# First attention: dense q and k projections, spread over the partitions through DRAM

## The chip, the cores and the metric

The kernel runs on one core of one Trainium2 chip. Its time is the device time of one execution in microseconds (us). Three runs of the kernel before took 4,061.84, 4,043.44 and 4,053.35 us; the median is 4,053.35. The profile shows one further execution, taken by the hardware profiler.

The engines are TensorE (PE, with its weight loads as PEld), VectorE (DVE), ScalarE (ACT), GpSimd (POOL) and SyncE (SP, whose queue issues the DMAs here).

## The reference

The network takes `x` of 2 batch rows, 1,024 tokens and 128 features, and runs eight sublayers over it, each on a layer norm of `x` and each added to `x`: a windowed attention (`attn_a`), a mixture of experts, a causal attention, the experts again, an attention with positions, a six-layer local-attention network, another attention, and the six-layer network again. The change is in the first sublayer, which is, cut to what matters:

```python
W, H = 64, 16; dh = D // H                       # D = 128, so dh = 8
q = x @ Wq.T + bq;  k = x @ Wk.T + bk;  v = x @ Wv.T + bv
kp = pad(k, W rows in front);  vp = pad(v, W rows in front)
idx = arange(C)[:, None] * W + arange(2 * W)[None, :]
scores = einsum('bcqhd,bckhd->bchqk', q by windows, kp[:, idx]) / sqrt(dh)
scores = where(idx >= W, scores, -1e9)
out = einsum('bchqk,bckhd->bcqhd', softmax(scores), vp[:, idx])
return out @ Wo.T + bo
```

Each window of 64 tokens looks at itself and the window before it, with 16 heads of 8 features. All arithmetic is in 32-bit floats.

## The kernel before

`x` is held transposed, features on the 128 partitions, as four blocks of 512 tokens (`self.xt`, two blocks for each batch row). Three early stages use the same small constants, loaded by `load_early` (L108): `self.w["a0"]` holds all weights of the first attention side by side.

`attn_a0` (L207) has two parts. The first part goes over the four blocks (L233 and L234). For each block:

- `norm` (L147) makes the layer norm. It transposes the block to token rows on PE (L158), takes means and variances on DVE (L162, L163), a root on ACT (L172) and a reciprocal on DVE (L173), scales four pieces on DVE (L181), transposes back on PE (L190) and copies the result to `xn` on ACT (L193).
- q and k are made for four groups `g` of four heads each (L236 to L246). A product gives one group: 128 output rows, of which head `j` of the group takes rows 32j to 32j + 7. The other 24 rows of each 32 are zero, since the weights were laid out so on the host (`spread`, L1780, in `_layout`). q leaves PSUM by way of ACT (L239), k by way of DVE (L244), into tiles `qT` and `kT`, indexed partition, group, token. So a block takes eight products, four for q and four for k.
- v is made with tokens on the partitions, in eight products of 128x128 (L250), and leaves by way of DVE (L254).

The PSUM tiles of the products (`pq`, `pk`, `pv`) share four buffers with the scores that follow. The order of the instructions in this part is the planner's own: it follows the program and takes an instruction ahead when its inputs are ready. On PE the order of a block is: transposes out of block k, transposes in of block k + 1, the products of q and k, and those of v.

The second part is `Chunks.run` (L834), under an order written out by the loop itself, the same on PE, ACT, DVE and POOL. It handles 16 chunks of 128 tokens, eight for each batch row. A chunk's `scores` (L854, products at L869) read q and k at partitions 32j to 32j + 7 only, one small product for each head and half; `softmax` (L874) subtracts the maxima on DVE and takes the exponential on ACT; `sums` (L886) normalises with POOL; then come transposes, the products with v (`outputs`, L907) and every four chunks the output product (`project`, L922). Chunks 0 to 3 read the first block of the first batch row, chunks 4 to 7 the second (and the last 64 keys of the first), and so on. PE reaches the scores of chunk 0 after the last product of v of the fourth block.

SP's queue is not in the written orders. It issues the loads of `x` (L128) and of the constants (L101) at the start; its next instructions belong to the experts' stage (L1097, L1102).

Of the kernel before, what the change touches and what calls it, by code (L numbers as in the profile page):

```python
# [10 lines left out]
F32 = mybir.dt.float32  # L11
BF16 = mybir.dt.bfloat16
AF = mybir.ActivationFunctionType
ALU = mybir.AluOpType
# [3 lines left out]
P = 128  # L18
B, N, D = 2, 1024, 128
# [6 lines left out]
HEADS, DH, WIN = 16, 8, 64  # L26
# [58 lines left out]
class Net:  # L85
# [118 lines left out]

    def attn_a0(self, key):  # L207
        nc, tc = self.nc, self.tc
        scale = 1.0 / math.sqrt(DH)
        with ExitStack() as ctx:  # L210
            wp = ctx.enter_context(tc.tile_pool(name="a0w", bufs=1))
            sb = ctx.enter_context(tc.tile_pool(name="a0s", bufs=2))
            ps = ctx.enter_context(tc.tile_pool(name="a0ps", bufs=2, space=PSUM))
            wp2 = ctx.enter_context(tc.tile_pool(name="a0av", bufs=1, space=PSUM))
            w, bv, mask = self.w["a0"], self.w["a0_bv"], self.w["a0_mask"]
            wqk = w[:, 0:1024].rearrange("p (s g e) -> p s g e", s=2, g=4)
            wv = w[:, 1024:1152]
            wo = w[:, 1152:1664].rearrange("p (g e) -> p g e", g=4)
            bqk = w[:, 1664:1672].rearrange("p (s g) -> p s g", s=2)
            bo = w[:, 1672:1673]  # L220

            def blk(b, k):
                return slice(WIN + 512 * k, WIN + 512 * (k + 1))

            xn, qT, kT, v = [], [], [], []
            for b in range(B):
                xn.append(wp.tile([P, WIN + N], F32, tag=f"xn{b}", name=f"a0xn{b}"))
                qT.append(wp.tile([P, 4, N], F32, tag=f"q{b}", name=f"a0q{b}"))
                kT.append(wp.tile([P, 4, WIN + N], F32, tag=f"k{b}", name=f"a0k{b}"))
                v.append(wp.tile([P, N // WIN, D], F32, tag=f"v{b}", name=f"a0v{b}"))  # L230
                nc.gpsimd.memset(xn[b][:, 0:WIN], 0.0)
                nc.gpsimd.memset(kT[b][:, :, 0:WIN], 0.0)
            for b in range(B):  # L233
                for k in range(2):  # L234
                    self.norm(self.xt[2 * b + k], xn[b][:, blk(b, k)], ps, f"{key}_{b}_{k}")
                    for g in range(4):  # L236
                        pq = ps.tile([P, 512], F32, tag="sc", name=f"a0pq{b}{k}{g}", bufs=4)
                        nc.tensor.matmul(pq, wqk[:, 0, g, :], xn[b][:, blk(b, k)], start=True, stop=True)
                        nc.scalar.activation(  # L239
                            qT[b][:, g, ts(k, 512)], pq, AF.Identity, bias=bqk[:, 0, g : g + 1]  # L240
                        )
                        pk = ps.tile([P, 512], F32, tag="sc", name=f"a0pk{b}{k}{g}", bufs=4)
                        nc.tensor.matmul(pk, wqk[:, 1, g, :], xn[b][:, blk(b, k)], start=True, stop=True)
                        nc.vector.tensor_scalar(  # L244
                            kT[b][:, g, blk(b, k)], pk, bqk[:, 1, g : g + 1], None, ALU.add
                        )  # L246
                    for c4 in range(2 * k, 2 * k + 2):
                        pv = ps.tile([P, 4, D], F32, tag="sc", name=f"a0pv{b}{c4}", bufs=4)
                        for c in range(4):
                            nc.tensor.matmul(  # L250
                                pv[:, c, :], xn[b][:, ds(WIN * (4 * c4 + c), 2 * WIN)], wv,
                                start=True, stop=True,
                            )
                        nc.vector.tensor_tensor(  # L254
                            v[b][:, ts(c4, 4), :], pv, bv[:, None, :].to_broadcast([P, 4, D]), ALU.add
                        )

            avs = [wp2.tile([P, 4, P], F32, tag=f"av{i}", name=f"a0av{i}") for i in range(2)]
            for av in avs:
                nc.vector.memset(av, 0.0)  # L260
            with tc.manual_schedule(engines=ORDERED):
                Chunks(self, qT, kT, v, wo, bo, avs, mask, scale, sb, ps).run()

# [1501 lines left out]
def _columns(v, width=P):  # L1767

    v = np.asarray(v)
    out = np.zeros((-(-v.size // width) * width,), v.dtype)  # L1770
    out[: v.size] = v
    return out.reshape(-1, width).T


def _layout(a):
    f = np.float32
    t = {"x": a["L0_attn_a_x"].reshape(T, D)}


    def spread(v):  # L1780
        out = np.zeros((4, 4, 32) + v.shape[1:], f)
        out[:, :, :DH] = v.reshape((4, 4, DH) + v.shape[1:])
        return out.reshape((4, P) + v.shape[1:])

    n = "L0_attn_a_"
    wqk = [spread(a[n + w]).transpose(2, 0, 1).reshape(P, 512) for w in ("Wq", "Wk")]
    t["a0"] = np.concatenate(
        wqk + [a[n + "Wv"].T, spread(a[n + "Wo"].T).transpose(1, 0, 2).reshape(P, 512)]
        + [spread(a[n + v]).T for v in ("bq", "bk")] + [_columns(a[n + "bo"])],
        1,  # L1790
    )
    t["a0_bv"] = a[n + "bv"].reshape(1, D)

    n = "L0_ffn_"
    w123 = [a[n + w].transpose(2, 0, 1).reshape(D, E * P) for w in ("w1", "w2", "w3")]
    sw3 = a[n + "sw3"].T.reshape(2, P, D).transpose(1, 0, 2).reshape(P, 2 * D)
    desc = np.tile(np.arange(E, 0, -1, dtype=f), (P, 1))
    t["f0"] = np.concatenate(
        w123 + [a[n + "sw1"].T, a[n + "sw2"].T, sw3, a[n + "gate_w"].T, a[n + "b1"].T, a[n + "b2"].T, desc,
         a[n + "b3"].T],  # L1800
        1,
    )
    t["b0"] = np.concatenate([a["L0_attn_b_wqk"], a["L0_attn_b_wov"]], 1)

    n = "L1_attn_a_"
    heads = np.repeat(np.eye(HEADS, dtype=f), DH, axis=0)
    t["a1"] = np.concatenate(
        [a[n + w] for w in ("Wq", "Wk", "Wv", "Wo")]
        + [_columns(a[n + "bq"]), _columns(a[n + "bo"])]
        + [np.tile(a[n + "pos_emb"][0, :, 0:3], (HEADS, 1)), heads],  # L1810
        1,
    )
    t["a1_rows"] = np.concatenate([a[n + v] for v in ("bq", "bk", "bv")]).reshape(1, 3 * D)

    n = "L1_attn_b_"

    t["b1_a"] = np.stack([np.repeat(a[n + m + "A"].transpose(1, 0, 2), 32, axis=0) for m in "qkvo"], 1)
    t["b1_s"] = np.stack([np.tile(a[n + m + "S"].transpose(1, 0, 2), (4, 1, 1)) for m in "qkvo"], 1)
    t["b1_gains"] = np.concatenate([a[n + "g1"], a[n + "b1"]]).reshape(1, 2 * D)
    t["b1_rows"] = np.concatenate([a[n + v] for v in ("qb", "kb", "vb")]).reshape(1, 3 * D)  # L1820
    t["b1_cols"] = np.concatenate([_columns(a[n + v]) for v in ("g1", "b1", "g2", "b2", "ob")], 1)

    for n in ("Wo", "W1", "W2"):
        t[n] = a[f"L1_ffn_{n}"]

    w = a["L1_ffn_Wqkv"]
    wv = w[:, :, 2 * INNER :].reshape(DEPTH, D, LH // 4, 2, 2 * LD).transpose(0, 1, 3, 2, 4)

    wqk = w[:, :, : 2 * INNER].reshape(DEPTH, D, 2, LH, 2, LD // 2).transpose(0, 1, 2, 4, 3, 5)
    t["Wqkv"] = np.concatenate(  # L1830
        [wqk.reshape(DEPTH, D, 2 * INNER), wv.reshape(DEPTH, D, INNER)], 2
    )
    qs, ks = a["L1_ffn_q_scale"], a["L1_ffn_k_scale"]
    roll = lambda v: np.roll(v, LD // 2, axis=-1)
    t["qk_scale"] = np.concatenate([qs, ks, roll(qs), roll(ks)], -1)
    b1 = a["L1_ffn_b1"]
    t["f1_cols"] = np.stack(
        [
            np.concatenate(
                [  # L1840
                    _columns(b1[i, :DI]), _columns(b1[i, DI:]), _columns(a["L1_ffn_ln_g"][i]),
                    _columns(a["L1_ffn_ln_b"][i]), _columns(a["L1_ffn_b2"][i]),
                ],
                1,
            )
            for i in range(DEPTH)
        ],
        1,
    )
    return t  # L1850
# [18 lines left out]
```

## Time and profile before

| what | value |
|---|---|
| median of three runs | 4,053.35 us (4,043.44 to 4,061.84) |
| the profiled execution's own time | 4,040.27 us |
| its span in the trace | 4,038.5 us |
| mean granted TensorE clock | 0.963 |
| start to the first norm's products (0 to 18.5 us) | PE busy 7.24 us |
| projections of the four blocks (18.5 to 58.9 us) | PE busy 39.25 us of 40.4 |
| chunk loop (58.9 to 232 us) | PE busy 130.74, DVE 136.22 of 173.1 us |
| everything after (232 to 4,038.5 us) | PE busy 3,684.7 us |

Times in the trace are from the span's start. A group or a piece of a timeline gives start, length, engine, line, operation, the tile written and the tiles read, and how many instructions were merged; in square brackets stands how long the engine had been idle and what ended the idle time. A row of windows gives the stretch, its length, the busy time of PE, PEld, DVE, ACT and POOL with the number of instructions, the granted TensorE clock, the busy share of the DMA engines and GB/s. The chain of waits goes back from the last instruction, at each step to what released it. A 32-bit product shows as two PE instructions.

### The profile page before, as it was taken

The page shows a single profiled execution, that of the slowest core. Times are in us where ns is not written, and L with a number is a line of the kernel's source. Part 1 is how long each engine was busy: PE and PEld are TensorE (multiplying, and loading weights), DVE is VectorE, ACT ScalarE, POOL GpSimd, SP SyncE. Part 2 cuts the span into 40 slices and gives each one's busy share as a digit, 9 for nine tenths or more (in the row PEclk, how much of TensorE's full clock was granted, in tenths as well). Part 3 has the DMA queues.
Part 4 walks back from the last instruction along what each step waited for, and adds up shares of the span by engine and source line. Part 5 has one row for each costly group of instructions (what it writes and reads, how often), then busy time and mean ns, then how long its engine had stood idle before and what let it go on. Part 6 is the DMA issues. An engine that isn't in the chain of part 4 may idle for free.

```text
span 4038.5 us, 156175 instructions
## 1 busy us (share of the span) xinstructions
PE 3861.9 (96%) x67340; PEld 2533.3 (63%) x67340; DVE 3140.5 (78%) x6016; ACT 2429.7 (60%) x4600; POOL 2495.8 (62%) x1614
## 2 busy tenths in 40 slices
PE   7889988999999999999999869999999999999998
PEld 4545544666666666666666536666666666666665
DVE  6866677787878787878788677787878787778786
ACT  3444435866666666666666448666666666566665
POOL 1333247776676766766766267766766767667662
PEclk8689888999999999999999879999999999999999
DMA  1011213332232333322222022333322323332222
GB/s 48 2 49 36 56 29 105 73 85 71 74 93 68 77 84 76 82 73 73 70 68 68 21 81 71 75 84 76 85 72 72 91 69 76 82 75 70 65 68 56
DMA packets 215541, 277.31 MB, mean 69 GB/s; under 512 B 52173, under 2 KB 108362, under 8 KB 214730
## 3 DMA queue, kind: packets, MB, share of 16 engines
q1 hardware_dynamic: 214858, 267.32, 25.9%
q8 instruction: 536, 8.78, 1.0%
q14 instruction: 147, 1.20, 0.1%
HBM read 67.76 MB, written 1.18 MB: 17 GB/s over the span
## 4 chain that ended last, share of the span: by engine, by line
PE 88%; DVE 6%; DMA 2%; ACT 1%; issue 1%; POOL 1%; SPq 0%; DVEq 0%; POOLq 0%; ACTq 0%
PE pj_l L1353 17%; PE y_l L1584 9%; PE pv_l L1455 9%; PE tqk_l L201 9%; PE av_l L1552 8%; PE sc_l L1502 7%; PE tpr_l L201 4%; PE to_l L201 4%; PE fg_l L1658 3%; PE fy_l L1694 3%; PE fa_l L1679 3%; PE sc_l L1493 2%; DMA f0share_e<-f0d_e 1%; PE f0F_e L1144 1%; PE f0S_e L1144 1%
## 5 line engine op out<-in xcount | busy, mean ns | idle before, releaser
L1382 DVE TENSOR_TENSOR t_l<-pj_l,rot_l 128x512 f32<-128x512 f32 x1536 | 968.3, 684 | 368.1 <-ACT sq_l L1362 356.5
L1399 POOL TENSOR_TENSOR raw_l<-t_l,t_l 128x1024 f32<-128x1024 f32 x384 | 909.0, 2367 | 532.5 <-DVE on_l L1560 307.1
L1353 PE MATMUL pj_l<-wqkv_l,x_l 128*128 128x512 f32 x1536 | 786.0, 614 | 7.0 <-DVE t_l L1382 4.8
L1414 POOL TENSOR_TENSOR raw_l<-raw_l,rn_l 128x1024 f32<-128x1024 f32 x384 | 723.7, 1903 | 94.7 <-ACT rn_l L1409 87.8
L1362 ACT ACTIVATE sq_l<-pj_l 128x512 f32<-128x512 f32 x768 | 462.4, 604 | 370.2 <-PE pj_l L1353 368.3
L1388 POOL TENSOR_TENSOR sq_l<-sq_l 128x512 f32<-128x512 f32 x384 | 491.5, 1280 | 311.2 <-ACT sq_l L1362 308.2
L201 PE MATMUL tqk_l<-ident_sb,raw_l 128*128 128x128 f32 x3072 | 453.1, 279 | 15.6 <-POOL raw_l L1414 13.6
L1432 ACT COPY qT_l<-tqk_l 128x512 f32<-128x512 f32 x384 | 225.3, 587 | 388.1 <-PE tqk_l L201 388.0
L201 PEld LDWEIGHTS tqk_l<-ident_sb,raw_l 128*128 128x128 f32 x3072 | 356.8, 142 | 160.6 <-issue 122.0
L1455 PE MATMUL pv_l<-wqkv_l,x_l 128*128 128x512 f32 x768 | 415.2, 623 | 5.7 <-DVE ln_xn_fl L1638 5.3
L1584 PE MATMUL y_l<-outT_l,wo_l 128*128 128x128 f32 x3072 | 393.7, 281 | 0.0
L1502 PEld LDWEIGHTS sc_l<-kT_l,qT_l 64*32 64x32 f32 x24576 | 294.7, 105 | 156.4 <-issue 146.0
L1584 PEld LDWEIGHTS y_l<-outT_l,wo_l 128*128 128x128 f32 x3072 | 357.5, 191 | 18.2 <-issue 1.0
L1552 PE MATMUL av_l<-vw_l,pT_l 64*32 64x64 f32 x24576 | 359.9, 224 | 6.0 <-issue 5.8
L1353 PEld LDWEIGHTS pj_l<-wqkv_l,x_l 128*128 128x128 f32 x1536 | 255.8, 192 | 172.6 <-issue 108.9
L1464 ACT COPY v_l<-pv_l 128x512 f32<-128x512 f32 x384 | 225.5, 587 | 222.4 <-PE pv_l L1455 201.7
L1560 DVE TENSOR_TENSOR on_l<-av_l,inv_l 128x512 f32<-128x512 f32 x384 | 247.5, 686 | 124.0 <-PE av_l L1552 123.7
L1552 PEld LDWEIGHTS av_l<-vw_l,pT_l 64*32 64x32 f32 x24576 | 294.0, 105 | 74.0 <-issue 67.6
L1502 PE MATMUL sc_l<-kT_l,qT_l 64*32 64x64 f32 x24576 | 329.1, 223 | 1.4 <-issue 1.4
L201 PEld LDWEIGHTS tpr_l<-ident_sb,pr_l 128*128 128x128 f32 x1536 | 188.9, 141 | 152.4 <-issue 117.5
L1512 DVE TENSOR_TENSOR pr_l<-sc_l,mx_l 128x512 f32<-128x512 f32 x384 | 265.6, 692 | 13.2
L1511 DVE TENSOR_REDUCE mx_l<-sc_l 128x8 f32<-128x512 f32 x384 | 261.6, 681 | 3.4 <-PE sc_l L1502 3.4
(321 smaller groups left out, 6177.7 us busy)
## 6 DMA issues: line engine op xcount, KB each, us to landing
vw_l<-v_l SPq DMA_DIRECT2D x3024, 64.0 KB
wqkv_l<-in_Wqkv SPq DMA_DIRECT2D x36, 512.0 KB
f0share_e<-f0d_e SPq DMA_DIRECT2D x64, 256.0 KB
rot_l<-in_rotary SPq DMA_DIRECT2D x24, 512.0 KB
wo_l<-in_Wo SPq DMA_DIRECT2D x12, 512.0 KB
w_l<-in_W SPq DMA_DIRECT2D x12, 341.0 KB
f_sb<-in_f SPq DMA_DIRECT2D x1, 1940.0 KB
qks_l<-in_qk_scale SPq DMA_DIRECT2D x12, 128.0 KB
```

Of the source, the lines that this page charges most:

```text
L201: self.nc.tensor.transpose(tp[:, c, :], src(c), self.ident)
L1353: self.nc.tensor.matmul(pj.rearrange("p h d -> p (h d)"), self.x[b][0][:, ts(a, P)], self.w[i]["qkv"][:, ds(INNER * s + 512 * u, 512)], st ...
L1362: self.nc.scalar.activation(st["sq", s][:, u], st["pj", s, u], AF.Square)
L1382: self.nc.vector.tensor_tensor(to, st["pj", s, u], tabs[:, k, None, ts(w, LD // 2)].to_broadcast(half), ALU.mult)
L1388: self.nc.gpsimd.tensor_tensor(sq[:, 0], sq[:, 0], sq[:, 1], ALU.add)
L1399: self.nc.gpsimd.tensor_tensor(r.rearrange("p h u d -> p u h d"), st["t1", s], st["t2", s], ALU.add)
L1414: self.nc.gpsimd.tensor_tensor(r, r, st["rn"][:, ts(s, LH), None].to_broadcast([P, LH, LD]), ALU.mult)
L1455: self.nc.tensor.matmul(pj, self.x[b][0][:, ts(a, P)], self.w[i]["qkv"][:, ds(2 * INNER + 512 * r, 512)], start=True, stop=True,)
L1502: nc.tensor.matmul(sc[j][ts(c, 32), hp, :], st["q"][rows, hp, ts(c, 32)], st["k"][rows, hp, ds(32 * c, 64)], start=False, stop=(hp == 7),)
L1512: nc.vector.tensor_tensor(p, st["sc"][j], mx[:, :, None].to_broadcast([P, 8, 64]), ALU.subtract)
L1552: nc.tensor.matmul(av[r][ts(c, 32), q, j, :], st["pT", j][rows, q, ts(c, 32)], st["vw"][rows, c, ts(2 * q + j, LD)], start=True, stop=True,)
L1584: self.nc.tensor.matmul(y[:, 0:P], self.w[i]["o"][:, c, :], st["o"][:, c, :], start=(c == 0), stop=(c == 7))
```

## The change

The weights of q and k are no longer spread with zero rows. They are laid out densely, 128 output rows for all 16 heads, in an order that puts head `j` of group `g` at rows 32j + 8g to 32j + 8g + 7. A block takes one product for q and one for k. Their results go, with the biases added (q on ACT, k on DVE as before), into one tile `both`. SP writes `both` to a DRAM tile `rows` in one DMA of 512 KB (128 partitions of 4 KB), and reads it back in eight DMAs of 64 KB, one for each of q and k and each `j`: 8 partitions, 4 groups, 512 tokens each. They land where the scores read: partitions 32j to 32j + 7 of a common tile `qk`, indexed partition, group, q or k, token. The other 24 partitions of each 32 are never written and never read. The weights' tile shrinks from 1,673 to 899 columns. `Chunks` gets views of `qk` in place of `qT` and `kT`; it is not changed itself.

```diff
             w, bv, mask = self.w["a0"], self.w["a0_bv"], self.w["a0_mask"]
-            wqk = w[:, 0:1024].rearrange("p (s g e) -> p s g e", s=2, g=4)
...
+            wqk = w[:, 0:256].rearrange("p (s e) -> p s e", s=2)
...
+            bqk, bo = w[:, 896:898], w[:, 898:899]
...
-                qT.append(wp.tile([P, 4, N], F32, tag=f"q{b}", name=f"a0q{b}"))
-                kT.append(wp.tile([P, 4, WIN + N], F32, tag=f"k{b}", name=f"a0k{b}"))
+                qk.append(wp.tile([P, 4, 2, WIN + N], F32, tag=f"qk{b}", name=f"a0qk{b}"))
...
-                    for g in range(4):
-                        pq = ps.tile([P, 512], F32, tag="sc", name=f"a0pq{b}{k}{g}", bufs=4)
-                        nc.tensor.matmul(pq, wqk[:, 0, g, :], xn[b][:, blk(b, k)], start=True, stop=True)
-                        nc.scalar.activation(
-                            qT[b][:, g, ts(k, 512)], pq, AF.Identity, bias=bqk[:, 0, g : g + 1]
-                        )
-                        pk = ps.tile([P, 512], F32, tag="sc", name=f"a0pk{b}{k}{g}", bufs=4)
-                        nc.tensor.matmul(pk, wqk[:, 1, g, :], xn[b][:, blk(b, k)], start=True, stop=True)
-                        nc.vector.tensor_scalar(
-                            kT[b][:, g, blk(b, k)], pk, bqk[:, 1, g : g + 1], None, ALU.add
-                        )
+                    both = sb.tile([P, 2, 512], F32, tag="both", name=f"a0both{b}{k}")
+                    for s in range(2):
+                        pr = ps.tile([P, 512], F32, tag="sc", name=f"a0pp{b}{k}{s}", bufs=4)
+                        nc.tensor.matmul(pr, wqk[:, s, :], xn[b][:, blk(b, k)], start=True, stop=True)
+                        if s == 0:
+                            nc.scalar.activation(both[:, s, :], pr, AF.Identity, bias=bqk[:, 0:1])
+                        else:
+                            nc.vector.tensor_scalar(both[:, s, :], pr, bqk[:, 1:2], None, ALU.add)
+                    rows = dr.tile([P, 2, 512], F32, tag="rows", name=f"a0rows{b}{k}")
+                    nc.sync.dma_start(rows, both)
+                    for s in range(2):
+                        for j in range(4):
+                            nc.sync.dma_start(
+                                qk[b][ds(32 * j, DH), :, s, blk(b, k)],
+                                rows[ts(j, 32), s, :].rearrange("(g d) t -> d g t", g=4),
+                            )
...
-                Chunks(self, qT, kT, v, wo, bo, avs, mask, scale, sb, ps).run()
+                Chunks(self, [x[:, :, 0, WIN:] for x in qk], [x[:, :, 1, :] for x in qk], v, wo, bo, avs, mask, scale, sb, ps).run()
...
+    dense = lambda v: v.reshape((4, 4, DH) + v.shape[1:]).swapaxes(0, 1).reshape(v.shape)
+    wqk = [dense(a[n + w]).T for w in ("Wq", "Wk")]
```

More of the change, by code (lines that the diff above doesn't have):

```diff
@@ L214, in attn_a0 @@
             wp2 = ctx.enter_context(tc.tile_pool(name="a0av", bufs=1, space=PSUM))
+            dr = ctx.enter_context(tc.tile_pool(name="a0d", bufs=4, space=bass.MemoryType.DRAM))
             w, bv, mask = self.w["a0"], self.w["a0_bv"], self.w["a0_mask"]
-            wqk = w[:, 0:1024].rearrange("p (s g e) -> p s g e", s=2, g=4)
[L217 to L220, printed above, removed]
+            wqk = w[:, 0:256].rearrange("p (s e) -> p s e", s=2)
+            wv = w[:, 256:384]
+            wo = w[:, 384:896].rearrange("p (g e) -> p g e", g=4)
+            bqk, bo = w[:, 896:898], w[:, 898:899]
             def blk(b, k):
                 return slice(WIN + 512 * k, WIN + 512 * (k + 1))
-            xn, qT, kT, v = [], [], [], []
+            xn, qk, v = [], [], []
             for b in range(B):
                 xn.append(wp.tile([P, WIN + N], F32, tag=f"xn{b}", name=f"a0xn{b}"))
-                qT.append(wp.tile([P, 4, N], F32, tag=f"q{b}", name=f"a0q{b}"))
-                kT.append(wp.tile([P, 4, WIN + N], F32, tag=f"k{b}", name=f"a0k{b}"))
+                qk.append(wp.tile([P, 4, 2, WIN + N], F32, tag=f"qk{b}", name=f"a0qk{b}"))
                 v.append(wp.tile([P, N // WIN, D], F32, tag=f"v{b}", name=f"a0v{b}"))
                 nc.gpsimd.memset(xn[b][:, 0:WIN], 0.0)
-                nc.gpsimd.memset(kT[b][:, :, 0:WIN], 0.0)
+                nc.gpsimd.memset(qk[b][:, :, 1, 0:WIN], 0.0)
             for b in range(B):
@@ L1785, in _layout @@
     n = "L0_attn_a_"
-    wqk = [spread(a[n + w]).transpose(2, 0, 1).reshape(P, 512) for w in ("Wq", "Wk")]
+    dense = lambda v: v.reshape((4, 4, DH) + v.shape[1:]).swapaxes(0, 1).reshape(v.shape)
+    wqk = [dense(a[n + w]).T for w in ("Wq", "Wk")]
     t["a0"] = np.concatenate(
         wqk + [a[n + "Wv"].T, spread(a[n + "Wo"].T).transpose(1, 0, 2).reshape(P, 512)]
-        + [spread(a[n + v]).T for v in ("bq", "bk")] + [_columns(a[n + "bo"])],
+        + [_columns(dense(a[n + v])) for v in ("bq", "bk")] + [_columns(a[n + "bo"])],
         1,
```

## The prediction, made before the changed kernel ran

> **What bounds the kernel now.** I read the busy times of the page first, then the chain of waits at the end of the first attention's projections, then that stretch's groups and windows, and last the DMA issues of other stages as rows for what is new.
>
> ```profile
> PE 3861.9 (96%) x67340; PEld 2533.3 (63%) x67340; DVE 3140.5 (78%) x6016; ACT 2429.7 (60%) x4600; POOL 2495.8 (62%) x1614
> ```
>
> and the windows of the first stage's two parts:
>
> ```profile
> 18.50:58.90 40.40, 39.25 (x152) 22.24 (x151) 24.61 (x62) 14.71 (x23) 0.00 (x0) 1.00 0.07 27
> 58.90:232.00 173.10, 130.74 (x2346) 95.17 (x2345) 136.22 (x192) 75.16 (x112) 61.64 (x36) 0.69 0.01 2
> ```
>
> [...]The projections last 40.4 us, PE busy for 39.25 of them; DMA is almost idle. In the chunk loop behind them DVE is busiest (136.2 of 173.1 us). The change edits the first of these rows; the other 99% of the kernel only moves.
>
> ```profile
> 48.90 0.45 PE ln_out_e L190 x4
> 49.35 0.02 issue
> 49.38 0.60 ACT a0xn L193
> 49.97 0.04 issue
> 50.02 1.13 PE a0pq L238 x2
> 51.14 0.86 PE a0pk L243 x2
> ...
> 57.15 1.80 PE a0pv L250 x16
> ...
> 59.72 1.16 PE a0sc L869 x57
> ```
>
> This is the chain through the fourth block (start, length). It stays on PE, with one ACT copy of 0.60 us. A product of 128x512 is two instructions, 0.86 us together. No evacuation of q or k (L239, L244) stands on the chain, so only the products can give time back directly.
>
> **What is removed.** Of 8 products a block, 6 go: 24 in all. At 0.858 us (eight products from 50.02 to 57.15 less the first one's 0.27 start) that is 20.6 us on the path. The 12 evacuations less on ACT (0.69 us) and on DVE (0.75 us) are worth 0 by themselves; PE covers them.
>
> **What then limits a block.** Block to block is 10.03 us now (L190 at 28.68, 38.71, 48.74). After: transposes out 0.45, copy with hand-overs 0.67, two products 1.99, values 1.80: 4.9 us of PE. Beside it runs the norm of the next block: statistics 1.24, root 0.30, reciprocal 0.18, four scalings of 0.37, with one k evacuation (0.75) and up to two value evacuations (0.69 each) among them on the same DVE queue. Counted from the first transposes out: statistics run from 1.1 to 2.3, the root behind the q evacuation on ACT ends between 2.7 and 3.1, the scalings end at 4.5 to 5.8. They are wanted at 4.9, so blocks 2 and 3 lose 0 to 0.9 us each. Block 1 loses nothing (its scalings end near 22, PE comes to it at 23.7), and the fourth block has no norm behind it. I take 1.1 us for both, ends 0 and 1.8. Gain on PE: 20.6 - 1.1 = 19.5 us. The first scores (L869) would stand at 58.9 - 19.5 = 39.4 us. The weights' load is 387 KB shorter (1,673 to 899 columns of 128 rows): nothing, since the chain at 16.38 to 18.54 waits for the norm.
>
> **What is added: 4 writes and 32 reads on SP's queue.** That queue is empty between 14.8 and 247 us (its next is L1097 in the next stage), so nothing useful stands behind its waits. The early loads have landed by then:
>
> ```profile
> 14.00:16.00 2.00, 0.00 (x0) 0.00 (x0) 0.27 (x2) 1.58 (x2) 0.00 (x0) 1.00 1.10 428
> 20.00:22.00 2.00, 2.00 (x4) 0.77 (x3) 0.96 (x4) 0.96 (x2) 0.00 (x0) 1.00 0.76 272
> 22.00:24.00 2.00, 2.00 (x6) 0.87 (x5) 1.67 (x4) 0.69 (x1) 0.00 (x0) 1.00 0.00 1
> ```
>
> DMA runs at up to 428 GB/s until about 21.5 us and stops. Block 0's k evacuation ends at 22.7. These rows, of the chain, the timeline at the kernel's end and the timeline of the later layers (start, length on the queue), price the transfers:
>
> ```profile
> 1.20 3.10 DMA xin<-in_x
> ```
>
> ```profile
> 4030.76 4.46 SPq L145 DMA_DIRECT2D out<-xout  x4
> 4033.26 0.69 DVE L144 COPY xout<-xoutp 128x512 f32<-128x512 f32 x1 [1.97 <-DMA out<-xout]
> ```
>
> ```profile
> 1504.88 0.59 SPq L1472 DMA_DIRECT2D vw_l<-v_l  x1
> 1505.51 0.60 SPq L1475 DMA_DIRECT2D vw_l<-v_l  x1
> ```
>
> A write of 256 KB to DRAM is through 2.5 us after its issue (30.76 to 33.26); ours has 512 KB, and 256 KB more at some 250 GB/s make it 3.5 us: it lands at 22.75 + 3.5 = 26.3 us. Eight reads of 64 KB follow, 0.36 us each to issue (the broadcast loads of the next stage, L1102, median) to 0.59 (above): 2.9 to 4.7 us. Landing of the last: 3.1 us by the 256 KB read of x, up to 5.1 by L1102 (issued at 248.80, used at 253.93). So block 0 is in place between 26.3 + 2.9 + 3.1 = 32.3 and 26.3 + 4.7 + 5.1 = 36.1 us; I take 34, as the transfers are as small as those of L1472. Scores of chunk 0 need only block 0 and come at 39.4: hidden, with 5 us of cover. With the cover gone each microsecond is one on the path. Block 1's chain on SP ends about 8 us later (42); chunk 4, its first reader, has its scores 32.6 us behind chunk 0's now (91.45 against 58.86), so at 72. Blocks 2 and 3 land near 58; chunk 8 (126.67 now) comes at 107. What a late block 0 would delay is the PE queue: the first scores wait, behind them every product of the chunk loop, and DVE's softmax for them.
>
> A rule of the Trainium skill speaks against such transfers: DMA: Bandwidth & Descriptors (Rules for kernel authors) says that under 64 KB one pays mostly overhead, and[...] that a DMA uses as many engines as divide the slowest dimension of both sides: 8 of 16 for these reads of 8 partitions. By its fixed cost of about 2.0 us, were all eight paid one behind the other, the reads take 16 us or more and end at 42, so 3 us are lost and the gain is 16.5. The rows of L1472 show issues 0.6 us apart without a wait for the landing before, so I sum with 19.5. No row here shows a DMA confined to 8 partitions.
>
> **The clock.** A second rule: TensorE: Matmul & The Clock Gate (Part 4) says that transposes do not count as activity for the gate. The part of a block that counts falls from about 8.9 of 10.0 us to 3.8 of 4.9. In the trace:
>
> ```profile
> 28.00:30.00 2.00, 1.76 (x17) 1.52 (x15) 1.62 (x4) 0.59 (x1) 0.00 (x0) 1.00 0.00 0
> 60.00:62.00 2.00, 1.27 (x60) 0.82 (x44) 1.11 (x2) 0.00 (x0) 0.00 (x0) 1.00 0.03 8
> 62.00:64.00 2.00, 0.38 (x3) 0.28 (x2) 1.93 (x4) 0.00 (x0) 0.00 (x0) 0.58 0.00 0
> ```
>
> The stretch with eight transposes and a copy wait (28 to 30) leaves the products behind it at 0.86 us; the clock falls to 0.58 only where PE is idle for most of 2 us. The new block has no idle of over 0.8 us. Where the rule won, a product would take the 1.95 us of the first cold one (18.66), 16 value instructions 3.9 (16 times the 0.24 of a cold transpose in the 1.94 us for 8), and a block 10.2 us: the gain shrinks to the first and perhaps second block's, 5 to 10 us. I sum with the warm rows.
>
> **Sum.** 20.6 - 1.1 - 0 (transfers) = 19.5 us from the profiled execution of 4,040.27 us (span 4,038.5): 4,020.8. The runs' median is 4,053.35, 13 us above that execution; taken from it, 4,033.8, said as **4,034 us**. The runs spread from 4,043 to 4,062, so about 0.5% (20 us) is what a measurement tells from no change, and the forecast of -0.48% lies at that edge.
>
> **Rivals.**
> 1. *A late block 0*: reads wait on one another in part (the halves for q and k go to the same 8 partitions, interleaved), or the first scores wait for both blocks of the first batch row. Against it: the unbroken issues above. Both blocks in place at 42 to 50 us instead of 39.4: gain 9 to 17, time 4,036 to 4,044, middle 4,040.
> 2. *The clock stays low in the projections*: 4,043 to 4,048, middle 4,046. Against it: the row 28 to 30.
> 3. *Slower: every read waits for the landing of the one before, and the scores for both blocks.* 26.3 + 8 x (0.4 + 2.6) = 50.3; second write 3.5; 24 more: 77.8 us. The scores start 18.9 us later than now: 4,072. It decides once a chained read costs over (58.9 - 26.3 - 3.5)/16 = 1.8 us. For it: 2.5 to 3.1 us from issue to use is what the rows show of one transfer. Against it: again L1472, which fills one tile in pieces without such waits.
> 4. *The shift is lost behind*: the chunk loop goes in and out of the low clock (0.69 granted), so its 173 us may come out 5 us longer or shorter: 4,029 to 4,039.
>
> **Chances.** Forecast 0.62, with a range of its own of 4,024 to 4,044 (runs' spread); rival 1 0.13, rival 2 0.07, rival 3 0.10, rival 4 0.08. Faster by over 0.5% (below 4,033): just under half of the forecast's share and of rival 4's, plus a little of rival 1: 0.40. Slower by over 0.5% (above 4,074): somewhat under half of rival 3, and other mishaps: 0.08. The rest, 0.52, lies between. The range of 8 in 10 takes in the forecast, rivals 1, 2 and 4, and the spread of the runs: 4,018 to 4,056; half of the rest is rival 3, the other half a shorter chunk loop or a fast set of runs.
>
> **What would show it.** Right: L190 every 5.0 to 5.8 us; products still 0.86 us from the third on; the first L869 at 39 to 41 us with no wait on the spread reads; the chunk loop 173 us long as now. Wrong: an idle PE ahead of L869 put down to a DMA (rivals 1 and 3, told apart by gaps between SP's read issues); granted clock near 0.5 between 24 and 40 us (rival 2); the first scores at 39 us and yet the next stage less than 15 us ahead of its 232 us of now (rival 4).

## The result, and the profile after

The changed kernel takes 4,014.95 us (median of 6 runs, 4,011.29 to 4,026.26); the kernel before, beside it, 4,049.54 us (6 runs, 4,042.12 to 4,061.84). The ratio is 0.993, with a 95% interval of 0.9912 to 0.9948, so the change is faster by over 0.5%. The forecast was -0.48%, with 4,034 us and a range of 4,018 to 4,056: the time came out 3 us below that range, and "faster by over 0.5%" had a chance of 0.40 against 0.52 for "same". Two more comparisons, told below, gave 0.9957 and 0.9941.

The profiled execution took 4,017.42 us with a span of 4,015.3, which is 23.2 us less than the span before. The page's first line and the windows of the first stage's two parts, projections and chunk loop, in the columns explained above:

```profile
PE 3837.7 (96%) x67292; PEld 2518.4 (63%) x67292; DVE 3132.5 (78%) x6004; ACT 2418.4 (60%) x4588; POOL 2492.4 (62%) x1614
```

```profile
18.60:42.70 24.10, 21.12 (x101) 13.73 (x100) 14.68 (x49) 6.46 (x11) 0.00 (x0) 0.93 0.57 143
42.70:208.71 166.01, 116.44 (x2346) 84.64 (x2345) 136.50 (x192) 75.19 (x112) 61.73 (x36) 0.81 0.07 12
```

PE runs 48 instructions less, DVE and ACT 12 evacuations less each. The first scores (now L874) stand at 42.70 us instead of 58.86: 16.2 us won in the projections. The chunk loop takes 166.0 us instead of 172.9, at a granted clock of 0.81 instead of 0.69, though nothing in it was edited. What comes behind takes 3,806.6 us, before 3,806.7. So 16.2 of the 23.2 us lie where the change was made, and 6.9 in a loop whose clock differs.

The chain of waits of the kernel after, from the second block's products on (start, length):

```profile
24.30 1.98 PE a0pp L239 x4
26.28 0.91 PE a0pv L255 x8
...
27.21 0.69 DVE a0v L259
27.91 0.32 DVE ln_xn_e L181
28.22 0.60 DVE a0v L259
28.82 0.33 DVE ln_xn_e L181
...
29.20 0.98 PE ln_out_e L190 x3
...
30.84 1.14 PE a0pp L239 x2
...
35.71 0.98 PE ln_out_e L190 x3
36.69 0.02 issue
36.71 0.59 ACT a0xn L193
...
37.35 3.64 PE a0pp L239 x4
40.99 1.80 PE a0pv L255 x16
```

Two things differ from the forecast block of 4.9 us. The chain leaves PE for DVE between the blocks: products start at 24.30, 30.84 and 37.35, 6.5 us apart. And the last block's two products took 3.64 us where the second block's took 1.98. The reason for the first is in DVE's timeline (start, length, engine, line, operation, tiles; in brackets its own idle time and what ended it):

```profile
33.00 0.75 DVE L243 TENSOR_SCALAR a0both<-a0pp,a_sb 128x512 f32<-128x512 f32 x1
33.66 0.40 DVE L181 TENSOR_SCALAR ln_xn_e<-ln_in_e,ln_mv_e,ln_rs_e 128x128 f32<-128x128 f32 x1
33.98 1.35 DVE L259 TENSOR_TENSOR a0v<-a0pv,a_bv_sb 128x512 f32<-128x512 f32 x2
35.25 1.04 DVE L181 TENSOR_SCALAR ln_xn_e<-ln_in_e,ln_mv_e,ln_rs_e 128x128 f32<-128x128 f32 x3
```

DVE does one scaling of the next block's norm, then both evacuations of the values (1.35 us), and only then the other three scalings. PE's next transposes wait for those. DVE is 61% busy in this stretch (14.68 of 24.10 us); so it looks like the order of its queue rather than its load that stops PE, which an experiment below tests.

The transfers, on SP's queue (start, length on the queue):

```profile
22.26 0.33 SPq L245 DMA_DIRECT2D a0rows<-a0both  x1
24.90 2.72 SPq L248 DMA_DIRECT2D a0qk<-a0rows  x8
28.09 6.07 SPq L245 DMA_DIRECT2D a0rows<-a0both  x2
35.48 10.63 SPq L248 DMA_DIRECT2D a0qk<-a0rows  x16
```

The blocks are counted from 0 here, as in the prediction's part on transfers. The first read is issued 2.6 us behind the write (forecast 3.5), and eight reads take 2.72 us to issue, 0.34 each. By the trace's record of landings they land one after another, the first at 28.0 and the last at 34.3 us, so block 0 is in place 8.4 us ahead of the first scores. Block 1's reads are issued from 35.5 us on: their own write, issued at 28.09 in the midst of block 0's reads, lands only at 35.4 by the same record. That costs nothing, since chunk 4, their first reader, comes at about 75 us. No instruction of PE waits for a DMA ahead of the first scores.

### The profile page after: what moved, and what is told of

The parts are those of the page before. It is cut to its first block, busy times and chain, and to the rows that moved or that the text cites. A ratio compares the mean times of both kernels' runs of the same rounds, so it can differ in the third digit from the quotient of the medians.

```text
span 4015.3 us, 156131 instructions
## 1 busy us (share of the span) xinstructions
PE 3837.7 (96%) x67292; PEld 2518.4 (63%) x67292; DVE 3132.5 (78%) x6004; ACT 2418.4 (60%) x4588; POOL 2492.4 (62%) x1614
## 3 DMA queue, kind: packets, MB, share of 16 engines
q8 instruction: 536, 8.78, 0.9%
## 4 chain that ended last, share of the span: by engine, by line
PE 86%; DVE 7%; DMA 2%; ACT 2%; issue 1%; POOL 1%; SPq 0%; DVEq 0%; POOLq 0%; ACTq 0%
PE pj_l L1358 17%; PE y_l L1589 9%; PE pv_l L1460 9%; PE tqk_l L201 9%; PE av_l L1557 8%; PE sc_l L1507 7%; PE tpr_l L201 4%; PE to_l L201 4%; PE fy_l L1699 3%; PE fg_l L1663 3%; PE fa_l L1684 3%; PE sc_l L1498 2%; DMA f0share_e<-f0d_e 1%; DVE a0pr L887 1%; DVE a0mx L886 1%
```

## The experiments

Three theories stood against one another. The first: the time comes from the products that went from PE's path, with the DMA hidden. The second: the chunk loop itself became faster with the new layout of q and k. The third: DMA or clock took part of the gain in the projections. All ratios are to the kernel before, run on the same chip in the same session.

### The two kernels again

No edit. The question is what belongs to the change and what to the clock in the loop.

> The kernel before, once more, for a second profile of it. Three theories of where more than the forecast 19.5 us comes from: (A) only the earlier end of the projections is real (16 us in the profiles), and the rest is chance in how often the clock is low; (B) the chunk loop (first scores to the first transposes out of the experts' stage: 173 us before, 166 after) runs with a higher clock in every execution, because of when and how it is entered; (C) it is shorter because of the new layout of q and k or the DMAs. A: the loop anywhere from 163 to 175 us, first scores at 58.9. B and C: 171 to 175 again.

> The changed kernel, once more. First scores at 42.7 us in all theories. A: the loop anywhere from 163 to 175 us. B and C: 164 to 168 us again, ratio to before 0.991 to 0.995.

The kernel before took 4,039.37 us (10 runs) against 4,040.17 (19 runs) for itself: 1.0003 [0.9991, 1.0015]. The changed kernel took 4,022.07 (4 runs): 0.9957 [0.9941, 0.9973]. The windows of the chunk loop, first of the kernel before:

```profile
59.27:225.18 165.91, 120.90 (x2345) 88.81 (x2345) 135.72 (x191) 75.31 (x112) 61.47 (x35) 0.76 0.01 2
```

and of the changed one:

```profile
42.15:217.83 175.68, 131.81 (x2346) 95.49 (x2345) 135.84 (x192) 75.31 (x112) 62.23 (x36) 0.70 0.07 12
```

Here the kernel before has the short loop (165.9 us, clock 0.76) and the changed one the long one (175.7, 0.70): the opposite of the first pair. DVE has the same work in both, 135.7 and 135.8 us. So the length of the loop goes with the clock of an execution, not with the kernel, and the 6.9 us of the first pair don't count for the change. The first scores stand at 59.27 and 42.15: 17.1 us, as before.

### The removed products put back, the rest of the change kept

```diff
-                        nc.tensor.matmul(pr, wqk[:, s, :], xn[b][:, blk(b, k)], start=True, stop=True)
+                        for _ in range(4):
+                            nc.tensor.matmul(pr, wqk[:, s, :], xn[b][:, blk(b, k)], start=True, stop=True)
```

Each dense product is made four times, so that PE does as many as before; layout, transfers and evacuations are those of the change.

> The changed kernel with each dense product of q and k done four times over, so that PE's work in the projections is that of before, and layout and transfers are those of after. First scores near 59 us in all theories. A: time as before within 0.2%. B: loop 171 to 175 us as before, ratio 0.998 to 1.002. C: loop 164 to 168 us and time 7 us or more under before, ratio 0.996 to 0.998.

Measured: 4,038.73 us (10 runs), 0.9994 [0.9981, 1.0007]. Its windows:

```profile
18.50:58.43 39.93, 38.78 (x150) 21.99 (x148) 15.45 (x49) 6.84 (x12) 0.00 (x0) 1.00 0.34 90
58.43:232.71 174.28, 131.10 (x2346) 95.62 (x2345) 136.79 (x192) 75.30 (x112) 61.78 (x36) 0.70 0.06 10
```

The first scores stand at 58.43 us, where the kernel before has them at 58.86 and 59.27, and the whole gain is gone. DVE and ACT have 9 and 8 us less to do than before in this stretch (15.45 against 24.61, 6.84 against 14.71), and that is worth under a microsecond. So the gain is that of the products on PE; the layout, the evacuations and the transfers together bring or cost less than a microsecond up to the first scores, and nothing that the whole times tell.

### The transfers left out

```diff
-                nc.gpsimd.memset(qk[b][:, :, 1, 0:WIN], 0.0)
+                nc.gpsimd.memset(qk[b], 0.0)
...
-                    rows = dr.tile([P, 2, 512], F32, tag="rows", name=f"a0rows{b}{k}")
-                    nc.sync.dma_start(rows, both)
...
-                            nc.sync.dma_start(
-                                qk[b][ds(32 * j, DH), :, s, blk(b, k)],
-                                rows[ts(j, 32), s, :].rearrange("(g d) t -> d g t", g=4),
-                            )
```

The products and evacuations stay, but q and k never reach the scores, whose operands are zero. That gives the bound of what the transfers can cost.

> The changed kernel without the DRAM write and the eight reads: the tile that the scores read is set to zero at the start, so q and k never reach the scores. If the transfers are hidden, first scores at 42.7 us and the time of the changed kernel within 0.2% (ratio to before 0.991 to 0.995). If they cost something (contention, waits in the loop), it is faster than the changed kernel by what they cost, 3 us or more.

Measured: 4,020.63 us (4 runs), 0.9951 [0.9936, 0.9966], beside 0.9957 with the transfers. The window of its projections:

```profile
18.50:42.23 23.73, 20.76 (x102) 13.64 (x101) 15.34 (x50) 6.43 (x11) 0.00 (x0) 0.93 0.09 31
```

The first scores stand at 42.23 us, as with the transfers (42.15 to 43.00 in three profiles). The DMA share falls from 0.57 to 0.09 and the time stays. Up to the first scores the transfers are hidden, and the missing 3 us of the projections' gain are not theirs; the granted clock of the projections is 0.93 here too. One small cost behind the first scores is told with the stages below.

### The clock in the chunk loop held up, in both kernels

```diff
-            tp = self.net.to_psum(self.ps, "tp", lambda g: st["p"][:, 4 * j + g, :], f"a0tp{m}_{j}")
+            tp = self.ps.tile([P, 4, P], F32, tag="tp", name=f"a0tp{m}_{j}")
+            if j == 2 * half:
+                self.nc.tensor.matmul(
+                    tp.rearrange("p c d -> p (c d)"), self.net.ident, self.net.xt[m // 4], start=True, stop=True
+                )
+            for g in range(4):
+                self.nc.tensor.transpose(tp[:, g, :], st["p"][:, 4 * j + g, :], self.net.ident)
```

Ahead of the transposes of each half chunk PE makes one product whose result is overwritten by them. PE has slack in this loop, and the added work should keep its clock up, so that the two kernels can be compared without that chance.

> The kernel before with one unused product (128x512, overwritten at once) ahead of the transposes in each half of a chunk, to keep PE busier in the chunk loop. If the loop's 166 to 176 us are the granted clock, and the product keeps it up, the loop takes 163 to 168 us with every output product's wait near 2.4 us, the same as in the changed kernel with the same products. If the products only add work, the loop is 170 to 185 us. First scores at 59.

> The same unused products in the changed kernel. With the clock held in both, the chunk loop is the same as in the kernel before with these products (within 2 us), and the two differ by the start of the first scores alone: 16 to 17 us. If the layout or the DMAs change the loop, it is shorter or longer by over 3 us here.

Measured: 4,033.44 us (10 runs), 0.9989 [0.998, 0.9999], for the kernel before with the added products, and 4,013.66 (4 runs), 0.9934 [0.992, 0.9949], for the changed one with them. The window of the loop, of the kernel before and then of the changed one, both with the added products:

```profile
59.75:224.96 165.21, 127.64 (x2409) 81.28 (x2408) 134.68 (x191) 74.92 (x112) 61.93 (x35) 0.93 0.01 2
```

```profile
43.76:209.98 166.22, 129.65 (x2410) 83.01 (x2409) 135.41 (x192) 74.77 (x112) 62.22 (x36) 0.91 0.07 12
```

With the clock at 0.91 to 0.93 the loops are 165.2 and 166.2 us: the new layout does not make the loop faster. The first scores are 16.0 us apart (59.75 and 43.76). The medians are 19.8 us apart, about 4 us more than the stage shows.

### The next block's norm ahead of the values

```diff
-                    self.norm(self.xt[2 * b + k], xn[b][:, blk(b, k)], ps, f"{key}_{b}_{k}")
+                    if b == k == 0:
+                        self.norm(self.xt[0], xn[0][:, blk(0, 0)], ps, f"{key}_0_0")
...
+                    n = 2 * b + k + 1
+                    if n < NBLK:
+                        self.norm(self.xt[n], xn[n // 2][:, blk(n // 2, n % 2)], ps, f"{key}_{n // 2}_{n % 2}")
                     for c4 in range(2 * k, 2 * k + 2):
```

The norm of block n+1 is written ahead of block n's value products, so that its scalings come before the values' evacuations on DVE. Nothing is added or left out.

> The changed kernel with the norm of the next block written ahead of the products of v, so that DVE takes the scalings before the evacuations of v. If those evacuations are what stretches a block to 6.2 and 6.5 us between the back transposes, the distances fall to 5.0 to 5.5 us and the first scores come at 39 to 40.5 us, not at 42.5: 2 to 3.5 us faster than the changed kernel, ratio to before 0.994 to 0.996. If the norm's own chain sets the distance, it stays at 6 or more and the first scores at 42.

Measured: 4,015.01 us (4 runs), 0.9939 [0.9923, 0.9954]. Its chain of waits, from the third block's norm on:

```profile
28.57 0.42 DVE ln_xn_e L181
...
29.04 1.30 PE ln_out_e L190 x4
30.34 0.02 issue
30.36 0.59 ACT a0xn L193
30.96 0.04 issue
31.00 1.98 PE a0pp L240 x4
...
36.24 1.98 PE a0pp L240 x4
38.22 1.80 PE a0pv L259 x16
```

The last two blocks' products are now 5.2 us apart instead of 6.5, the last block's products are no longer cold (1.98 us for its two), and the first scores stand at 39.93 us: within half a microsecond of the 39.4 that the prediction had worked out. That is 2.8 us earlier than in the changed kernel's profile, which the whole times alone could not tell. So the late scalings ahead of the last block and its cold products come from DVE's order. From the second block to the third the products are still 6.15 us apart (24.85 to 31.00): there the evacuations of k (0.75 us) and of values (0.68) still stand ahead of the scalings in the chain, and 1.3 us of that loss remain.

### Every read made twice

```diff
+                    spare = sb.tile([P, 4, 512], F32, tag="spare", name=f"a0spare{b}{k}", bufs=1)
                     for s in range(2):
                         for j in range(4):
                             nc.sync.dma_start(
+                                spare[ds(32 * j, DH), :, :],
+                                rows[ts(j, 32), s, :].rearrange("(g d) t -> d g t", g=4),
+                            )
+                            nc.sync.dma_start(
                                 qk[b][ds(32 * j, DH), :, s, blk(b, k)],
```

This takes the cover from the transfers, shows whether the reads are chained, and which blocks the first scores wait for.

> The changed kernel with each of the eight reads of a block preceded by a second one of the same bytes into a spare tile: the reads of block 0 then take 16 transfers of about 1 us (64 KB at the 60 to 70 GB/s that the windows show while only they run). If the scores wait for block 0 alone, it lands near 43 us and the first scores stay between 42.5 and 46 us: time within 0.1% of the changed kernel. If they wait for both blocks of the batch row, they start at 60 us or later and the gain is gone: ratio to before 0.999 to 1.003. A cover of 5 us, as forecast, would be used up in the first case.

Measured: 4,022.95 us (4 runs), 0.9955 [0.9941, 0.997]. SP's timeline, some of the sixteen reads of block 0 and what follows:

```profile
28.22 0.26 SPq L249 DMA_DIRECT2D a0spare<-a0rows  x1
29.46 0.26 SPq L253 DMA_DIRECT2D a0qk<-a0rows  x1
30.71 0.26 SPq L249 DMA_DIRECT2D a0spare<-a0rows  x1
...
36.79 0.27 SPq L253 DMA_DIRECT2D a0qk<-a0rows  x1
38.22 1.59 SPq L245 DMA_DIRECT2D a0rows<-a0both  x2
46.39 0.29 SPq L249 DMA_DIRECT2D a0spare<-a0rows  x1
```

The first eight reads go out 0.3 us apart, 25.25 to 27.68. From the ninth on (28.22) they come 0.9 to 2.0 us apart, 1.2 us each from the ninth to the eleventh. In this kernel that could be the edit's own doing, since the ninth read overwrites what the first one put into the spare tile. The changed kernel has no such tile, and its sixteen reads of blocks 1 and 2 do the same: eight go out 0.34 us apart, from 35.48 us on, and from the ninth on (38.64) each is issued 0.02 us after the read eight before it has landed (38.62 by the record of landings). SP's waits of the changed kernel up to 100 us name these landings (total, times, longest):

```profile
SPq L248 <- DMA a0qk<-a0rows: 6.2, 9, 0.8
```

The record counts the landings of this queue's DMAs on eight semaphores in turn. So the limit of eight under way may well be the program's own; that it is the chip's is not shown.

And the timeline of PE and ACT at the start of the scores:

```profile
43.83 0.43 PE L879 MATMUL a0sc<-a0qk 8*64 8x128 f32 x2 [0.43 <-DVE a0v L264]
46.38 0.69 ACT L241 ACTIVATE a0both<-a0pp,a_sb 128x512 f32<-128x512 f32 x1 [8.78 <-DMA a0rows<-a0both]
47.13 0.61 PE L879 MATMUL a0sc<-a0qk 8*64 8x128 f32 x18 [2.87 <-ACT a0both L241]
```

The scores start at 42.97 us, as without the added reads. That is ahead of block 1's reads, whose first issue is at 46.39, so they don't wait for both blocks. They then stop for 2.87 us, until ACT has evacuated the last block's q; scores and projections share their PSUM buffers. ACT had been idle for 8.78 us, and what ended that was the buffer a0both, held by a write that was issued behind the doubled reads and took 8.1 us to land, as the chain of waits has it:

```profile
38.22 8.08 DMA a0rows<-a0both
```

The last read of block 0 lands at 45.2 us by the record of landings, so the cover of the transfers is used up as well, but the buffer comes 2 us later and hides it. With twice the reads the first cost is thus a buffer held by a write behind the reads in its queue: some 3 us at this point, which the whole time does not show (0.9955 beside 0.9957).

### The best of these, and the change once more

The last kernels run the change, the norm put ahead, and the norm put ahead together with the loop's added products; the two edits are those shown.

> The changed kernel once more, in five rounds, because the first two comparisons differ (0.993 and 0.9957). If only the projections' 16 to 17 us are real, the ratio is 0.9955 to 0.9965; if the chunk loop gains too, 0.993 or less. First scores at 42 to 43 us; the loop anywhere from 163 to 176 us.

> The norm of the next block ahead of the products of v, once more, beside the changed kernel on the same chip. If the start of the scores (39.9 against 42.5) is all that it gives, it is 2 to 3 us faster than the changed kernel: 0.0005 to 0.0008 lower in the ratio.

> Both that order and the unused product in each half of a chunk. First scores at 39.9, loop 164 to 168 us: 4 to 10 us faster than the order alone, ratio to before 0.992 to 0.9945.

Measured, with 6 runs each against 4,040.56 us (11 runs) for the kernel before: the change 4,018.51 us, 0.9941 [0.992, 0.9963]; the norm ahead 4,014.53, 0.9933 [0.9915, 0.9951]; both edits 4,008.72, 0.9915 [0.9897, 0.9932], a little below what was expected. The change's interval takes in both of the cases that were to be told apart, so this comparison leaves open whether more than the projections' 16 to 17 us is real. The loop of the last:

```profile
39.04:204.81 165.77, 128.04 (x2410) 81.56 (x2409) 135.44 (x192) 74.92 (x112) 62.19 (x36) 0.93 0.08 13
```

It has both the early start (39.04 us) and the short loop, and its median is 9.8 us below the change's; five of the change's six runs are slower than all six of these, though the intervals of the two ratios overlap.

### The stages side by side

From each profile: the start of the first scores, the length of the chunk loop behind it with its granted clock, and what is left of the span (us).

| kernel | first scores at | loop | clock | rest |
|---|---|---|---|---|
| before | 58.86 | 172.9 | 0.69 | 3,806.7 |
| before, again | 59.27 | 165.9 | 0.76 | 3,813.0 |
| before, added products in the loop | 59.75 | 165.2 | 0.93 | 3,820.7 |
| products put back | 58.43 | 174.3 | 0.70 | 3,820.0 |
| after | 42.70 | 166.0 | 0.81 | 3,806.6 |
| after, again | 42.15 | 175.7 | 0.70 | 3,811.0 |
| after, third time | 43.00 | 168.2 | 0.76 | 3,801.4 |
| transfers left out | 42.23 | 167.4 | 0.75 | 3,809.5 |
| reads twice | 42.97 | 169.2 | 0.80 | 3,800.5 |
| after, added products in the loop | 43.76 | 166.2 | 0.91 | 3,804.9 |
| norm ahead | 39.93 | 173.9 | 0.71 | 3,807.7 |
| norm ahead, again | 39.86 | 166.5 | 0.78 | 3,805.4 |
| norm ahead, added products | 39.04 | 165.8 | 0.93 | 3,800.3 |

Only the first column goes with the edits. The second goes up and down by 10 us with the clock, in both kernels: 172.9 us and more at clocks of 0.69 to 0.71, 169.2 us and less from 0.75 on. The third varies by 20 us. Most of that lies in a later attention that no edit touches, `attn_b1`: from the first instruction on its input `b1in` to the next norm it takes 75.5 to 94.2 us, with short and long ones in both kernels.

The first column leaves out one small cost of the transfers. In the kernels without them DVE's first step of the softmax starts 2.0 us behind the first scores, in those with them 2.7 us (reads twice: 5.8). Where the transfers are left out, DVE evacuates the last block's k ahead of its values; in the changed kernel the planner has put it behind them, and most of chunk 0's scores wait for that PSUM buffer. First the kernel with the transfers left out, then the changed one:

```profile
40.55 0.75 DVE L243 TENSOR_SCALAR a0both<-a0pp,a_sb 128x512 f32<-128x512 f32 x1 [4.62 <-PE a0pp L239]
```

```profile
44.22 1.16 PE L874 MATMUL a0sc<-a0qk 8*64 8x128 f32 x58 [0.16 <-DVE a0both L243]
```

So 0.7 us of the 16 us at the first scores are given back at once. With the clock held up, the loops of the two kernels end 15.0 us apart (224.96 and 209.98).

## Why the prediction was right, and where its sizes were off

The mechanism held: the products came off PE's path, and the transfers stayed hidden. Of the signs named for it one held in full: PE shows no wait on the spread reads ahead of the first scores. The transposes back (L190) began 5.4 and 6.1 us apart instead of 5.0 to 5.8, the last block's products ran at half pace, the first scores stood at 42.7 us instead of 39 to 41, and the chunk loop took 166 us instead of 173.

**Products off the path: right.** With the products put back the gain is gone (0.9994). The 12 evacuations fewer on each of ACT and DVE were put at nothing, and the same run agrees: 0.4 to 0.8 us between its first scores and those of the two profiles of before.

**The norm of the next block: the term that was mis-sized.** The step said that "blocks 2 and 3 lose 0 to 0.9 us each" (counted from 1), 1.1 us together, because the scalings "end at 4.5 to 5.8" behind "up to two value evacuations". They end later. From the third block's first transpose (28.37) three of its four scalings of the next block end at 36.3, 7.9 us on. The transposes out that the count started from are themselves stretched, as they wait piece by piece for the scalings before; the root waits for ACT's q evacuation, and both value evacuations stand ahead of three scalings. Products came 6.54 and 6.51 us apart instead of 4.88: a loss of 3.3 us for the two blocks instead of 1.1, outside its end of 1.8. The norm put ahead took 1.7 us of that away; what is left is shown only as the chain has it, with k's evacuation and one of values ahead of the scalings.

**No idle PE of over 0.8 us, and a warm clock: wrong in small.** PE stood idle for 1.00 us and, after three transposes, for 0.68 us ahead of the last block's products. The windows of the kernel after:

```profile
36.00:37.00 1.00, 0.67 (x3) 0.28 (x2) 0.29 (x1) 0.29 (x1) 0.00 (x0) 1.00 0.47 131
37.00:38.00 1.00, 0.65 (x1) 0.50 (x2) 0.00 (x0) 0.30 (x1) 0.00 (x0) 0.65 0.57 66
38.00:39.00 1.00, 1.00 (x2) 0.34 (x1) 0.00 (x0) 0.00 (x0) 0.00 (x0) 0.50 0.48 68
```

The granted clock falls to 0.50 and the two products take 3.64 us instead of 1.98. So rival 2 (a low clock in the projections) came for one block and cost 1.7 us, not for all of them. It is a matter of the edge: with the same two waits (0.99 and 0.68 us) the second profile of the change has 1.98 us there, three of the other four with this order have 3.53 to 3.60 and one 2.78, and the order that shortens the first wait has none. The rule that transposes don't count as activity (TensorE: Matmul & The Clock Gate, Part 4 of the Trainium skill) is not settled by this. Between the third block's values and the last block's products lie 2.7 us of idle time and transposes alone, but the same is true of the block before, and there the products ran at 1.98 us.

**The sum of the projections.** The removed products give 20.6 us, as forecast. The first block gives 0.5 more: its products and the second's are 5.65 us apart where before they were 11.41, so 5.76 are won instead of a quarter of 20.6, less a start that is 0.1 later. The norm takes 3.3 away and the cold products 1.7. That makes 16.1 us, and 16.2 were measured, where the forecast had 19.5. With the norm put ahead, the first scores come at 39.93 and 39.86 us in two profiles, against the forecast's 39.4.

**The transfers: right.** Write and reads cost no time that the runs tell (0.9951 without, 0.9957 with), and 0.7 us by the profiles, behind the first scores. Issue of eight reads was put at 2.9 to 4.7 us and took 2.72; the write at 3.5 took 2.6. Block 0 was put in place at 34 us and is, at 34.3; in the two further profiles of the change at 35.2 and 34.5. The first scores come 7 to 8.5 us later, where a cover of 5 us was forecast.

What the forecast took from DMA: Bandwidth & Descriptors of the Trainium skill holds in one half. By its Rules for kernel authors the slowest dimension sets how many engines a DMA uses, 8 of 16 for these reads, and a share of about half of the DMA engines is what they show (0.53 to 0.54). Its fixed cost of about 2.0 us (section on the anatomy of one DMA, where it is given for DMAs issued from GpSimd; these are SP's) is not paid one behind the other: eight reads go out 0.34 us apart and land 0.9 us apart on average. So paid, the reads were to end at 42 us and take 3 us of the gain. The gain did come out 3 us short, but with the transfers left out it was as short; the agreement is chance.

**Rivals 1 and 3 (a late block 0): not so.** Both had the first scores wait for both blocks, or the reads for one another. In the kernel with every read doubled the scores start before block 1's reads are issued. The reads of a block do land one behind the other, but some 0.9 us apart; a chain in their issue shows only from the ninth on, at about 1.2 us each with the reads doubled, below the 1.8 from which rival 3 would have decided.

**Rival 4 (the shift lost behind): half right.** The loop's length does vary with its clock, by 166 to 176 us instead of the 5 us either way around 173 that it was given, and in the first profile it fell to the good side. The forecast said that the loop would stay at 173 us; there is no such fixed length.

**The level.** Of the 34.6 us between the medians of the first comparison 15 to 16 are shown to be the change's. The other comparisons have 18.1 us, 22.0 us and, with the added products, 19.8 us; between the kernel with the products put back and the change there are 16.7 us. In the first session the kernel before ran at 4,049.5 us, in the other three at 4,039 to 4,041: that is 9 us of the difference, and a forecast in microseconds from runs at 4,053 carries it along. The projections gave less than forecast and the first comparison more (-0.70% against -0.48%): that the total came out as near as it did is luck of the level, not a merit of the sum. Whether a few microseconds behind the first stage belong to the change stays open: profiles scatter by 20 us there, more than what is looked for.

## What to carry to other kernels

When work is taken from the busiest engine, lay out the whole queue of the engine that is next, in its order. Here DVE was 61% busy and its lateness still cost 3 us, and the waits then let PE's clock fall; half of the 3 us and the cold products came back when the scalings were put ahead of the value evacuations. The transfers through DRAM were all but free here, since the first reader came 7 us or more behind the last of block 0's; when you count on that, count the buffers that the writes hold too, since with slower reads these ran out. And where a stage's granted clock changes from one execution to the next, compare stage by stage from several profiles before a few microseconds are put down to an edit.

## What the runs showed of the hardware

The reads from DRAM to 8 partitions are slower than their share of engines says. One window of the kernel after, with block 0's write to DRAM from 128 partitions:

```profile
23.00:24.00 1.00, 1.00 (x10) 0.82 (x8) 0.79 (x2) 0.34 (x1) 0.00 (x0) 1.00 0.97 387
```

and two of the kernel with doubled reads, where there is nothing but these reads:

```profile
28.00:30.00 2.00, 1.17 (x7) 0.60 (x5) 2.00 (x6) 0.00 (x0) 0.00 (x0) 1.00 0.54 53
30.00:32.00 2.00, 1.76 (x8) 1.01 (x8) 1.14 (x9) 0.59 (x1) 0.00 (x0) 1.00 0.53 60
```

The last two columns are DMA share and GB/s. The write moves 387 GB/s at a share of 0.97, the reads 53 to 60 GB/s at a share of 0.53 to 0.54. Half the engines are busy (the record of landings counts eight for each read, sixteen for each write), and each moves about a quarter of what it does for the write: 53/0.54 = 98 to 60/0.53 = 113 GB/s for a full share, against 387/0.97 = 399. A read of 64 KB so takes 1.1 to 1.2 us of the queue when eight are under way, far more than the 0.34 us that its issue suggests. No run here separates what sets the reads apart from the write: the direction, pieces of 2 KB instead of 4 KB, and 8 partitions instead of 128.

And adding work to PE made a stage no slower, often faster: 32 products more (64 instructions) hold the granted clock of the chunk loop at 0.91 to 0.93 and its length at 165.2 to 166.2 us in three profiles, where without them ten profiles have 0.69 to 0.81 and 165.9 to 175.7 us.
